# Statistics of y by accumulating passes on ScalarE, and quarters of the image for the first block of k

## The chip, the cores and the metric

One core of a Trainium2 chip runs the whole program. The metric is the device time of the program in microseconds; the time before is a median of three runs.

## The reference

The input is x of 8 images with 384 channels and 64 x 64 positions. Two residual layers follow each other:

- Layer 0: x is normalised over groups of 12 channels. q, k and v are each a 1x1 convolution (384 to 384) and then a depthwise 3x3 convolution. In each of 8 heads of 48 channels, q and k are divided by their norm over the 4096 positions, the 48 x 48 products go through a softmax and are applied to v; a 1x1 convolution follows, and the result is added to x.
- Layer 1: the new x is normalised again over groups, and scanned in four directions with a selective scan of 16 states; the four results are added to y. Then y is normalised over its channels at every position and passed through gelu:

```python
mu = jnp.mean(yc, axis=-1, keepdims=True)
var = jnp.mean((yc - mu) ** 2, axis=-1, keepdims=True)
yc = (yc - mu) * jax.lax.rsqrt(var + LN_EPS) * ln_weight + ln_bias
y = jnp.transpose(yc, (0, 3, 1, 2)).astype(x.dtype)
return jax.nn.gelu(y, approximate=False)
```

and added to x. All is float32.

## The kernel before, in words

The images go one after the other. For each, `channel_attention` makes layer 0 and `selective_scan` makes the scan, which takes most of the time and writes y to DRAM, 4096 positions by 384 channels. The last part of layer 1, the normalisation of y, gelu and the sum, is not made behind the scan of its image but inside the attention of the next image; only that of the last image stands alone at the end, in `finish`.

In the attention the channels lie on the 128 partitions in three blocks (m = 0, 1, 2), each of 4096 columns. `conv` (line 207) makes one block, or some rows of it: TensorE multiplies chunks of 512 columns, three matmuls each (L223), into one of three PSUM buffers; ScalarE evicts each chunk with its bias (L228) into a tile `pre`, which has two buffers, and then multiplies it by the centre weight into the result (L232); VectorE adds the other eight taps (L244). A part of the rows needs one more row on each inner side. The first block of k is made in two halves (line 277), so that VectorE can begin before the whole block is there; blocks 1 and 2 of k are made whole, and so are blocks 0 and 1 of q. After a block, TensorE transposes it and ScalarE copies the transposes out (L268, L269), and ScalarE squares it in eight passes with an accumulator (L255) for the norm, whose small operations on VectorE and ScalarE are L258 to L261; `diag` (L283) spreads it by a matmul. For q, `lg` (L311) holds the logits.

`token_norm` (line 873) makes the mean and the variance of y for each position. It loads y in 16 pieces of 256 positions into a tile with three buffers (L881); VectorE makes two statistics of 384 columns for each piece (L884) and aggregates them (L885); at the end ScalarE takes the root (L886) and VectorE makes the scale and the shift (L887, L888). It is called in the attention of images 1 to 7 ahead of v (line 327), and in `finish` (line 920). `finish_part` (line 891) then applies scale and shift (L900), transposes, applies gelu (L908), adds x (L912) and stores.

In the scan most instructions are held in the order in which they are written. In the attention and in `token_norm` they are not: a scheduler places the instructions of each engine, by their dependences and its own estimates of time, when the program is built. The order that results is fixed, and each engine runs its own instructions in that order. SyncE issues all loads and stores named here, also in a fixed order.

Of the kernel before, what the change touches and what calls it, by code (L numbers as in the profile page):

```python
# [9 lines left out]
F32 = mybir.dt.float32  # L10
AF = mybir.ActivationFunctionType
ALU = mybir.AluOpType
# [3 lines left out]
P = 128  # L16
C = 384
NJ = C // P
H = W = 64
# [3 lines left out]
NT = L // P  # L23
# [31 lines left out]
BW = max(hi - lo for lo, hi in BANDS)  # L55
# [21 lines left out]
def tile_channel_attention_then_selective_scan(ctx: ExitStack, tc: tile.TileContext, a: dict):  # L77
    nc = tc.nc
# [14 lines left out]
    eps = const.tile([P, 1], F32, name="eps")  # L93
# [6 lines left out]
    for name in ("dt_bias", "Ds", "ln_w", "ln_b", "temp"):  # L100
        t = const.tile(list(a[name].shape), F32, name=name)
# [61 lines left out]
    def channel_attention(b, x, stats, before):  # L163
# [5 lines left out]
        with ExitStack() as st:  # L169
            wp = st.enter_context(tc.tile_pool(name=f"w{b}", bufs=1))  # L170
            work = st.enter_context(tc.tile_pool(name=f"a{b}", bufs=2))
# [78 lines left out]
            def inverse_norm(acc, tag):  # L250
                r = work.tile([P, 1], F32, tag="rn", bufs=4, name=f"rn{tag}")
                parts = work.tile([P, L // JUNK], F32, tag="rp", name=f"rp{tag}")
                for i in range(L // JUNK):
                    junk = work.tile([P, JUNK], F32, tag="junk", bufs=1, name=f"junk{tag}_{i}")
                    nc.scalar.activation(  # L255
                        junk, acc[:, bass.ts(i, JUNK)], AF.Square, accum_out=parts[:, i : i + 1]
                    )
                nc.vector.tensor_reduce(r, parts, AX.X, ALU.add)  # L258
                nc.vector.tensor_scalar_max(r, r, L2_EPS * L2_EPS)
                nc.scalar.activation(r, r, AF.Sqrt)  # L260
                nc.vector.reciprocal(r, r)  # L261
                return r

            def to_tokens(acc, t4, out, tag):

                pt = ps_t.tile([P, 4, P], F32, tag="pt", name=f"pt{tag}_{t4}")
                for i in range(4):
                    nc.tensor.transpose(pt[:, i, :], acc[:, bass.ts(4 * t4 + i, P)], ident)  # L268
                nc.scalar.copy(out, pt)  # L269
# [4 lines left out]
            rks = wp.tile([P, C], F32, name=f"rks{b}")  # L274
            for m in range(NJ):
                acc = work.tile([P, L], F32, tag="acc", name=f"ak{b}{m}")
                parts = (0, H // 2, H) if m == 0 else (0, H)
                for y0, y1 in zip(parts, parts[1:]):
                    conv("k", wk, bk, m, y0, y1, acc[:, y0 * W : y1 * W])
                for t4 in range(NT // 4):  # L280
                    to_tokens(acc, t4, kT[:, 4 * t4 : 4 * t4 + 4, bass.ts(m, P)], f"k{b}{m}")
                r = inverse_norm(acc, f"k{b}{m}")
                diag = work.tile([P, P], F32, tag="diag", name=f"diag{b}{m}")  # L283
                nc.vector.tensor_scalar_mul(diag, ident, r)
                pr = ps_a.tile([P, CH], F32, tag="pa", name=f"pr{b}{m}")
                nc.tensor.matmul(pr[:, :P], lhsT=ones, rhs=diag, start=True, stop=True)
                nc.scalar.copy(rks[:, bass.ts(m, P)], pr[:, :P])
# [4 lines left out]
            for m in range(NJ):  # L292
                lo, hi = BANDS[m]
                wd = hi - lo
                acc = work.tile([P, L], F32, tag="acc", name=f"aq{b}{m}")
                parts = (0, H // 2, H) if m == NJ - 1 else (0, H)
                for y0, y1 in zip(parts, parts[1:]):
                    conv("q", wq, bq, m, y0, y1, acc[:, y0 * W : y1 * W])
                pa = ps_a.tile([P, CH], F32, tag="pa", name=f"pa{b}{m}")
                for t4 in range(NT // 4):  # L300
                    qT = work.tile([P, 4, P], F32, tag="qT", name=f"qT{b}{m}_{t4}")
                    to_tokens(acc, t4, qT, f"q{b}{m}")
                    for i in range(4):
                        t = 4 * t4 + i
                        nc.tensor.matmul(
                            pa[:, :wd], lhsT=qT[:, i, :], rhs=kT[:, t, lo:hi],
                            start=t == 0, stop=t == NT - 1,
                        )
                r = inverse_norm(acc, f"q{b}{m}")
                nc.vector.tensor_mul(r, r, small["temp"][:, m : m + 1])  # L310
                lg = work.tile([P, BW], F32, tag="lg", name=f"lg{b}{m}")  # L311
                nc.vector.tensor_mul(lg[:, :wd], pa[:, :wd], rks[:, lo:hi])
                nc.vector.scalar_tensor_tensor(
                    lg[:, :wd], lg[:, :wd], r, mask[:, m, :wd], ALU.mult, ALU.add
                )
                mx = work.tile([P, 1], F32, tag="mx", name=f"mx{b}{m}")
                nc.vector.reduce_max(mx, lg[:, :wd], axis=AX.X)
                nc.vector.tensor_scalar_mul(mx, mx, -1.0)
                sm = work.tile([P, 1], F32, tag="sm", name=f"sm{b}{m}")
                nc.scalar.activation(lg[:, :wd], lg[:, :wd], AF.Exp, bias=mx, accum_out=sm)  # L320
                nc.vector.reciprocal(sm, sm)
                nc.vector.tensor_scalar_mul(attn[:, m, lo:hi], lg[:, :wd], sm)
# [3 lines left out]
            if before is not None:  # L326
                scale, shift = token_norm(b, wp, work, before[2])

                def emit(i):
                    t = work.tile([P, L], F32, tag="acc", name=f"fin{b}_{i}")  # L330
                    room = [t[:, n * FT * NJ : (n + 1) * FT * NJ] for n in range(3)]
                    finish_part(*before, i, scale, shift, room, ps_t, "pt")
# [30 lines left out]
            parts = (0, H // 2, 3 * H // 4, H)  # L363
# [508 lines left out]

    def token_norm(b, keep, work, y_d):

        mv = keep.tile([P, NT, 2], F32, name=f"fmv{b}")
        scale = keep.tile([P, NT], F32, name=f"fsc{b}")
        shift = keep.tile([P, NT], F32, name=f"fsh{b}")
        n = FT // P
        for i in range(L // FT):
            y = work.tile([P, n, C], F32, tag="ft", bufs=3, name=f"fy{b}_{i}")  # L880
            nc.sync.dma_start(y, y_d[bass.ts(i, FT), :].rearrange("(l p) c -> p l c", p=P))  # L881
            for t in range(n):
                stats = work.tile([P, nc.vector.BN_STATS_DIM], F32, tag="fst", name=f"fst{b}_{i}_{t}")
                nc.vector.bn_stats(stats, y[:, t, :])  # L884
                nc.vector.bn_aggr(mv[:, n * i + t, :], stats)  # L885
        nc.scalar.activation(scale, mv[:, :, 1], AF.Sqrt, bias=eps)  # L886
        nc.vector.reciprocal(scale, scale)  # L887
        nc.vector.scalar_tensor_tensor(shift, mv[:, :, 0], -1.0, scale, ALU.mult, ALU.mult)  # L888
        return scale, shift

    def finish_part(b, x1_d, y_d, i, scale, shift, room, psum, tag):
# [23 lines left out]
    def finish(b, x1_d, y_d):  # L915
        with ExitStack() as st:
            wp = st.enter_context(tc.tile_pool(name=f"fw{b}", bufs=1))
            work = st.enter_context(tc.tile_pool(name=f"f{b}", bufs=2))
            ps = st.enter_context(tc.tile_pool(name=f"fp{b}", bufs=4, space=PSUM))
            scale, shift = token_norm(B, wp, work, y_d)  # L920
            for i in range(L // FT):
                room = [
                    work.tile([P, FT * NJ], F32, tag=f"r{n}", bufs=4, name=f"fr{b}_{i}_{n}")
                    for n in range(3)
                ]
                finish_part(b, x1_d, y_d, i, scale, shift, room, ps, "pz")
# [3 lines left out]
    for b in range(B):  # L930
        x1, x1_d, stats1 = channel_attention(b, *x, before)
        y_d, x = selective_scan(b, x1, stats1)
        before = (b, x1_d, y_d)
# [50 lines left out]
```

## Time and profile before

| what | value |
|---|---|
| median of 3 runs | 20560.08 us (20553.85 to 20561.49) |
| profiled execution, its own time | 20559.6 us |
| span of that execution | 20557.8 us, granted TensorE clock 0.968 |
| VectorE busy | 19292.1 us (94%) |
| TensorE busy (matmul) | 19007.6 us (92%) |
| ScalarE busy | 17927.7 us (87%) |
| GpSimd busy | 15434.4 us (75%) |
| statistics of y on VectorE: L884, L885 | 256 of 546 ns (128 loads with two each), 256 of 173 ns |
| taps on VectorE, 128x4032, L244 | 4416 ns each |
| scans on VectorE, L570 | 12288, 1266 or 1230 ns each |

The times of groups are sums over the span, and many lie beside each other on different engines. An image's attention can be found in the profile by the names of its tiles: `ak` is a block of k, `aq` of q, with the image's number in the names of `pre` and `pc` (`pre1k`: image 1). The attention of image 1 begins near 2579 us; the end of the program, where nothing but the last image's normalisation is left, begins near 20453 us. In rows in order of time, the first number is the start in microseconds, the second the duration; brackets hold the idle time of the engine before, and what released it.

### The profile page before, as it was taken

How to read it: one execution, taken by the hardware profiler on the slowest of the kernel's cores; microseconds unless marked ns; L12 is line 12 of the kernel's file. 1: busy time of each engine (PE TensorE's matmuls, PEld its weight loads, DVE VectorE, ACT ScalarE, POOL GpSimd, SP SyncE). 2: the span in 40 equal slices, each digit the busy share in tenths (PEclk: the TensorE clock that was granted, in tenths of full speed). 3: DMA queues.
4: the chain of work that ended last, by engine and by line, in shares of the span. 5: the costliest groups of instructions: out<-in, count | busy, mean ns of one | idle time of the engine just before them, and what ended most of it. 6: DMA issues, size and time to landing. Idle time of an engine off the chain costs nothing. (4 is left out here: it accounts for less than half of the span.)

```text
span 20557.8 us, 319218 instructions
## 1 busy us (share of the span) xinstructions
PE 19007.6 (92%) x118000; PEld 10494.5 (51%) x118000; DVE 19292.1 (94%) x17310; ACT 17927.7 (87%) x32267; POOL 15434.4 (75%) x6918
## 2 busy tenths in 40 slices
PE   7999979999899998999989999899998999989998
PEld 4555545555455554555545555455554555545554
DVE  8999989999899998999989999899998999989998
ACT  3999949999599995999959998599985999859998
POOL 0999809998199981999819997199971999729997
PEclk8999989999899998999989999899998999989999
DMA  1222322223223232222322223222232222322223
GB/s 40 80 91 93 101 77 82 92 92 100 74 83 92 92 104 69 83 91 92 106 69 83 92 92 104 71 83 92 92 102 72 84 92 92 99 74 84 92 92 117
DMA packets 953162, 1807.94 MB, mean 88 GB/s; under 512 B 125904, under 2 KB 646352, under 8 KB 945456
## 3 DMA queue, kind: packets, MB, share of 16 engines
q1 hardware_dynamic: 950736, 1787.40, 27.1%
q8 instruction: 931, 15.25, 0.3%
q14 instruction: 631, 5.17, 0.1%
q10 hardware_dynamic: 864, 0.12, 0.0%
HBM read 1468.39 MB, written 318.77 MB: 87 GB/s over the span
## 5 line engine op out<-in xcount | busy, mean ns | idle before, releaser
L558 POOL TENSOR_TENSOR db<-w,B 128x1536 f32<-128x1536 f32 x4088 | 14145.7, 3470 | 524.1 <-DVE h L570 193.7
L570 DVE TENSOR_TENSOR_SCAN h<-da,ca,db 128x512 f32<-128x512 f32 x10752 | 13030.9, 1266 | 413.8 <-issue 238.2
L604 ACT ACTIVATE hc<-pt,ct 128x384 f32<-128x384 f32 x15128 | 8430.7, 579 | 237.4 <-PE pt L592 176.4
L549 ACT ACTIVATE da<-dt,neg_a 128x512 f32<-128x512 f32 x12288 | 8509.4, 696 | 100.2 <-DVE h L570 66.9
L592 PE MATMUL pt<-ident,h 128*128 128x128 f32 x49152 | 7978.3, 287 | 524.5 <-ACT hc L604 346.0
L592 PEld LDWEIGHTS pt<-ident,h 128*128 128x128 f32 x49152 | 5143.4, 140 | 5174.3 <-ACT hc L604 2506.3
L621 PE MATMUL py<-hc,pair 128*64 128x384 f32 x24576 | 5328.0, 512 | 9.2 <-DVE ys L692 9.2
L406 POOL MEMSET wdt<- 128x1536 f32 x8 | 11.0, 1378 | 3612.3 <-DMA x1d<-x 3612.3
L570 DVE TENSOR_TENSOR_SCAN h<-da,db 128x512 f32<-128x512 f32 x1536 | 1807.3, 1230 | 129.9 <-ACT da L549 61.2
L628 PE MATMUL py<-hc,pair 128*64 128x128 f32 x24576 | 1897.5, 280 | 0.0
L621 PEld LDWEIGHTS py<-hc,pair 128*64 128x64 f32 x24576 | 1215.4, 135 | 1042.6 <-issue 1042.6
L455 PE MATMUL px<-x,wx 128*44 128x128 f32 x6144 | 1502.6, 338 | 35.3 <-ACT x L421 29.1
L628 PEld LDWEIGHTS py<-hc,pair 128*64 128x64 f32 x24576 | 1403.3, 136 | 252.5 <-issue 248.7
L533 POOL TENSOR_TENSOR w<-x,dt 128x512 f32<-128x512 f32 x744 | 1058.1, 1422 | 0.0
L455 PEld LDWEIGHTS px<-x,wx 128*44 128x44 f32 x6144 | 635.0, 121 | 818.1 <-issue 772.6
L584 POOL COPY ca<-h 128x6 f32<-128x6 f32 x1792 | 348.7, 195 | 699.3 <-DVE h L570 690.5
L606 DVE TENSOR_SCALAR hc<-pt,ct 128x384 f32<-128x384 f32 x1256 | 739.0, 605 | 57.2 <-PE pt L592 15.4
L515 PE MATMUL pd<-xd,wdt 128*128 128x512 f32 x1536 | 747.1, 609 | 44.8 <-ACT hc L604 39.0
L353 PE MATMUL pp<-v,mT 128*128 128x512 f32 x1152 | 557.6, 638 | 124.1 <-DVE v L244 57.3
L525 ACT ACTIVATE dt<-pd,dt_bias 128x512 f32<-128x512 f32 x768 | 474.4, 685 | 19.7 <-PE pd L515 16.0
L515 PEld LDWEIGHTS pd<-xd,wdt 128*128 128x128 f32 x1536 | 275.5, 193 | 327.3 <-issue 187.8
L353 PEld LDWEIGHTS pp<-v,mT 128*128 128x128 f32 x1152 | 230.1, 206 | 405.4 <-issue 316.4
(315 smaller groups left out, 11369.7 us busy)
## 6 DMA issues: line engine op xcount, KB each, us to landing
B<-bcd SPq DMA_DIRECT2D x2048, 512.0 KB
yd<-ys SPq DMA_DIRECT2D x128, 576.0 KB
ys<-yd SPq DMA_DIRECT2D x256, 288.0 KB
yd<-ys SPq DMA_DIRECT2D x256, 288.0 KB
x<-in_x SPq DMA_DIRECT2D x48, 1024.0 KB
x1d<-x SPq DMA_DIRECT2D x192, 256.0 KB
fy<-yd SPq DMA_DIRECT2D x128, 384.0 KB
fin<-yd SPq DMA_DIRECT2D x112, 384.0 KB
```

The lines of the kernel that those rows point to most:

```text
L353: nc.tensor.matmul(pc, lhsT=mT[:, j, bass.ts(m, P)], rhs=v[:, j, bass.ts(c, CH)], start=j == 0, stop=j == NJ - 1,)
L455: pin(nc.tensor.matmul(split(pxs[s][:XR, :])[:, part, :], lhsT=wx[:, j, k, :], rhs=view(x1[j], k, c)[:, part, :], start=i == 0, stop=i == ...
L515: pin(nc.tensor.matmul(pds[j], lhsT=wdt[:, k, bass.ts(j, P)], rhs=xds[s], start=True, stop=True))
L533: pin(eng.tensor_mul(split(ws[s][:, j, :]), view(x1[j], k, c), split(dts[s][:, j, :])))
L549: pin(nc.scalar.activation(t, dts[s][:, j, :], AF.Exp, scale=neg_a[:, j, k, n : n + 1]))
L558: pin(eng.tensor_mul(t, ws[g // NP], bts[g][:, v : v + 1, :].broadcast_to([P, NJ, CH])))
L570: pin(nc.vector.tensor_tensor_scan(h, da, db, 0.0 if start else carries[s - 1][:, j, n : n + 1], ALU.mult, ALU.add,))
L592: pin(nc.tensor.transpose(t[:, bass.ts(j, P)], h2s[g][:, j, bass.ts(q, HP), :].rearrange("p l v -> p (l v)"), ident))
L604: pin(eng.activation(out, src, AF.Copy, scale=scale))
L606: pin(eng.tensor_scalar_mul(out, src, scale))
L621: pin(nc.tensor.matmul(py[f * HP : (f + 1) * HP, lb, :C], lhsT=pair, rhs=hc[:, f, :], **flags))
L628: pin(nc.tensor.matmul(py[f * HP : (f + 1) * HP, j, C:], lhsT=pair, rhs=hc[:, f, bass.ts(j, P)], **flags,))
```

## The change

Two things change. The first block of k is made in three parts, two quarters of the image and then the second half, instead of two halves. And in `token_norm` the statistics of VectorE are replaced by passes of ScalarE: for each piece of y, two passes with Identity whose accumulator gives the sum of 384 channels, one multiplication by -1/384 on VectorE for both, and two passes with Square, with minus the mean as bias, whose accumulator gives the sum of the squared deviations. The root at the end takes the division by 384 as its scale. All passes write to one tile `junk` that is not read. The tiles `diag` and `lg` get one buffer instead of two.

```diff
             for m in range(NJ):
                 acc = work.tile([P, L], F32, tag="acc", name=f"ak{b}{m}")
-                parts = (0, H // 2, H) if m == 0 else (0, H)
+                parts = (0, H // 4, H // 2, H) if m == 0 else (0, H)
...
-                diag = work.tile([P, P], F32, tag="diag", name=f"diag{b}{m}")
+                diag = work.tile([P, P], F32, tag="diag", bufs=1, name=f"diag{b}{m}")
...
-                lg = work.tile([P, BW], F32, tag="lg", name=f"lg{b}{m}")
+                lg = work.tile([P, BW], F32, tag="lg", bufs=1, name=f"lg{b}{m}")
...
     def token_norm(b, keep, work, y_d):
 
-        mv = keep.tile([P, NT, 2], F32, name=f"fmv{b}")
...
             nc.sync.dma_start(y, y_d[bass.ts(i, FT), :].rearrange("(l p) c -> p l c", p=P))
+            junk = work.tile([P, C], F32, tag="fj", bufs=1, name=f"fj{b}_{i}")
+            ts = slice(n * i, n * i + n)
             for t in range(n):
-                stats = work.tile([P, nc.vector.BN_STATS_DIM], F32, tag="fst", name=f"fst{b}_{i}_{t}")
-                nc.vector.bn_stats(stats, y[:, t, :])
-                nc.vector.bn_aggr(mv[:, n * i + t, :], stats)
-        nc.scalar.activation(scale, mv[:, :, 1], AF.Sqrt, bias=eps)
+                g = n * i + t
+                nc.scalar.activation(junk, y[:, t, :], AF.Identity, accum_out=shift[:, g : g + 1])
+            nc.vector.tensor_scalar_mul(shift[:, ts], shift[:, ts], -1.0 / C)
+            for t in range(n):
+                g = n * i + t
+                nc.scalar.activation(
+                    junk, y[:, t, :], AF.Square, bias=shift[:, g : g + 1],
+                    accum_out=scale[:, g : g + 1],
+                )
+        nc.scalar.activation(scale, scale, AF.Sqrt, bias=eps, scale=1.0 / C)
         nc.vector.reciprocal(scale, scale)
-        nc.vector.scalar_tensor_tensor(shift, mv[:, :, 0], -1.0, scale, ALU.mult, ALU.mult)
+        nc.vector.tensor_mul(shift, shift, scale)
         return scale, shift
```

In the changed file the multiplication on VectorE is L889, the passes are L888 and L892, and the root is L896.

## The prediction

> **What bounds the kernel now.** I read first the page: busy time and the chain of work that ended last. The chain names ACT, DVE, PE and POOL in the scan, each by a few per cent, so no single engine bounds the whole. The order of instructions in the scan is the same in both programs on all engines (VectorE's 14,248 instructions of that stage, ScalarE's 29,256, and those of PE and SyncE), so I leave the scan at its time and price only the two places that the change touches: the attention at the head of each image and the end of the program.
>
> The attention, read in VectorE's order of time. Image 0 has no statistics of y, image 1 has them; columns are start, duration, engine, line, operation, count and the idle time before it.
>
> ```profile
> 31.83 0.18 DVE L142 RECIPROCAL rstd<-rstd 128x3 f32<-128x3 f32 x1 [0.27 <-ACT rstd L141]
> 53.12 36.49 DVE L244 SCALAR_TENSOR_TENSOR ak<-pre0k,dwk,ak 128x1953 f32<-128x1953 f32 x16 [21.11 <-ACT ak L232]
> 95.58 0.16 DVE L258 TENSOR_REDUCE rnk<-rpk 128x1 f32<-128x8 f32 x1 [5.97 <-ACT junkk L255]
> ...
> 102.21 60.98 DVE L244 SCALAR_TENSOR_TENSOR ak<-pre0k,dwk,ak 128x3969 f32<-128x3969 f32 x14 [5.47 <-ACT ak L232]
> ...
> 174.01 4.35 DVE L244 SCALAR_TENSOR_TENSOR aq<-pre0q,dwq,aq 128x3969 f32<-128x3969 f32 x1 [1.58 <-ACT aq L232]
> ```
>
> ```profile
> 2599.11 1.02 DVE L884 BATCH_NORM_STATS2 fst<-fy 128x6 f32<-128x384 f32 x2 [0.79 <-DMA fy<-yd]
> 2600.34 2.25 DVE L244 SCALAR_TENSOR_TENSOR ak<-pre1k,dwk,ak 128x1953 f32<-128x1953 f32 x1 [0.20 <-ACT ak L232]
> ...
> 2640.70 0.55 DVE L884 BATCH_NORM_STATS2 fst<-fy 128x6 f32<-128x384 f32 x1
> ...
> 2649.61 60.98 DVE L244 SCALAR_TENSOR_TENSOR ak<-pre1k,dwk,ak 128x3969 f32<-128x3969 f32 x14 [3.16 <-ACT ak L232]
> ...
> 2720.88 13.20 DVE L244 SCALAR_TENSOR_TENSOR aq<-pre1q,dwq,aq 128x3969 f32<-128x3969 f32 x3 [1.05 <-ACT aq L232]
> ```
>
> See that from the first tap of k to the first tap of q image 0 takes 174.01 - 53.12 = 120.9 us without statistics and image 1 takes 2720.88 - 2600.34 = 120.5 us with them. VectorE's statistics therefore cost nothing here: they lie in the 20 us before the first tap and in the gap before block 1 of k. What sets both waits is the chain PE, eviction (L228), centre tap (L232): block 1 starts at 102.21 and 2649.61, 49.1 and 49.3 us after the first tap, though the taps of block 0 take only 36.5 us. The reason is the two buffers `pre`: ScalarE can evict for block 1 only when the first half is released.
>
> The end of the program, VectorE's and ScalarE's order of time:
>
> ```profile
> 20464.50 1.02 DVE L884 BATCH_NORM_STATS2 fst<-fy 128x6 f32<-128x384 f32 x2 [8.84 <-DMA fy<-yd]
> ...
> 20493.47 0.30 DVE L885 BATCH_NORM_AGGREGATE fmv<-fst 128x2 f32<-128x6 f32 x2
> ```
>
> ```profile
> 20452.84 1.28 ACT L886 ACT_TABLE_LOAD   x1
> 20493.81 0.32 ACT L886 ACTIVATE fsc<-fmv,eps 128x32 f32<-128x32 f32 x1 [39.68 <-DVE fmv L885]
> 20494.98 1.91 ACT L900 ACTIVATE fr<-fr,fsh,fsc 128x384 f32<-128x384 f32 x3 [0.85 <-DVE fsh L888]
> ```
>
> Here nothing covers the statistics: from 20464.50 to 20493.81, 29.3 us for 16 loads of y, ScalarE only waits (39.68 us), with its table for Sqrt already in.
>
> **What the Trainium skill says.** "ScalarE: Activation LUTs", section "What ACT_TABLE_LOAD costs": an ACTIVATE with immediate scale and bias takes 186 + 0.833 N ns, a pointer operand adds about 93 ns, and successive ones overlap by about 93 ns; a table load takes 1283 ns and a drain of about 1380 ns follows. The trace agrees on the first: the accumulating Square at L255 over 512 columns has a mean of 632 to 649 ns against 613 estimated. It agrees on the 1283 ns; no drain of 1380 ns shows (the load at 20496.90 is followed by an ACTIVATE at 20498.20). The page does not price the accumulator; the trace does (next part).
>
> **The change, part by part.**
>
> *1. A pass with accumulator.* No row has it at 384 columns. L255 at 512 columns:
>
> ```profile
> 2639.66 0.63 ACT L255 ACTIVATE junkk<-ak 128x512 f32<-128x512 f32 x1 [0.78 <-DVE fmv L885]
> 2640.20 0.19 ACT L255 ACTIVATION_READ_ACCUMULATOR junkk<-ak 128x1 f32 x1
> 2640.42 0.63 ACT L255 ACTIVATE junkk<-ak 128x512 f32<-128x512 f32 x1
> ```
>
> So one with its read takes 0.76 us from start to start. 128 columns fewer are 0.107 us (slope of L232: (3.71 - 2.00)/2048 = 0.835 ns per column): 0.65 us for the sum pass, and 0.75 for the Square with its pointer bias (an estimate with that page's 93 ns). Mean 0.70; bounds 0.60 and 0.85 (the L255 of 512 columns with a pointer). Per image 64 passes, 45 us of ScalarE.
>
> *2. Image 0: quarters alone.* The first quarter needs 17 rows: two chunks of 512 and one of 64. Chunks leave PE every 2.57 us; the second one's eviction is at 45.12, the small one's follows to 46.1, the tap over 1024 columns takes 1.15 (L232 in v): first tap at 47.3 instead of 53.12, 5.8 us earlier. Sixteen taps of 1.27 (the 128x1008 rows of v), some overlapping, end about 67.2. The price: one more chunk, of 128 columns, and eight more taps at half size, whose fixed cost is in these 1.27 us (two of 1008 against one of 2016 at 2.25 to 2.31). The third part needs the first quarter's buffer (free at about 60), but its evictions stand behind the q bias, which waits for PE to about 61.6; its centre tap ends about 69.4, so VectorE stands 2 us and ends block 0 at 87.5. Block 1 takes the second quarter's buffer, free at 67.2 (before: the first half's, about 78); PE's chunks then run to 88.7, two transposes' evictions and a Square follow, the centre tap ends at 95.5. Block 1 starts 102.2 - 95.5 = 6.7 us earlier. The norm's small operations (0.8 us), before in the gap, now stand between taps: 5.9 us won.
>
> *3. Images 1 to 7: quarters with the passes.* ScalarE's order now has 7 passes before the first centre tap, 4.9 us. They fit beside PE, which delivers the chunks at 2589.8 and 2592.3: first centre tap ends at 2595.0, 5.3 us before 2600.34. From the third part's tap (ends about 2616.5) to block 1's tap there stand 18 passes, 6 evictions, 4 Squares and 5 copies: 12.6 + 4.2 + 2.8 + 2.8, with the last wait on VectorE and the tap's 3.71: I follow it item by item to 2644.9, against 2649.6: 4.7 us. VectorE's removed statistics (32 of 0.546 and 32 of 0.173 us, 23 us) give nothing, as image 0 against image 1 shows. It gets 16 multiplications of 128x2 instead (0.15 us, as L259), each waiting for two passes; queued behind each are the taps, and PE's transposes wait for those. Eight stand before block 1's start, in slack; eight after it cost 1.2; the norm's operations 0.8; short waits for the pass where the multiplications of y loads 13 and 14 stand in q's taps 0.3. 4.7 - 2.3 = 2.4 us per image, 16.8 for seven. Bounds: 0.5 and 5.3 (the whole first lead).
>
> Of what moves: SyncE's loads of y now wait for ScalarE's passes, the last ones in q's block 1 instead of by 2630; queued behind are the load of wv (now ahead of the last four, needed about 2665, released about 2656) and those of the first finished parts, which start at 2808.99. So nothing. Single buffers for `diag` and `lg`: their matmul and softmax are done tens of us before the next, 0; if one were late, under 1 us. Table loads: 578 in both.
>
> *4. The end.* ScalarE makes all 64 passes alone: per load 2 x 0.65 + 2 x 0.75 = 2.8, and once to VectorE and back: 0.15 with about 0.15 of waking (between 0.03 and 0.24 by the gaps at 20494): 3.1 us. 16 x 3.1 = 49.6 against 29.3: +20.3. The Sqrt table load now stands behind the passes, in the open: +1.3. In all +21.6. The loads of y do not bind: 16 of them and 8 for the parts to finish went out from 20461 to 20489 before, 1.2 us each. The 60 us of finishing that follow keep their order. Bounds 16 (passes at 0.60, 0.2 of waking) and 27 (0.85 on half of them, 0.45).
>
> *Sum.* -5.9 - 16.8 + 21.6 = -1.1 us on the profiled execution's 20559.6 us (its span 20557.8 and 1.8 around it). That execution is 0.5 us under the median 20560.08; 20559 us for the median after.
>
> **The rivals.**
> - A, the sum as above: 20559, chance 0.66.
> - B, the lead is kept whole: 5.3 in each of seven images, 6.7 in image 0, the end only 16 us longer: -28, 20532. For it: block 1 waits on a chain that begins earlier. Against: ScalarE's passes are in that chain. Chance 0.22.
> - C, VectorE is what bounds the attention and all that is taken from it counts: after the first tap of image 1 stand about 7.4 us of statistics (10 of 0.546, 11 of 0.173), with the lead 12.7 us per image: -88.9 - 5.9 + 21.6 = -73, 20487. Against: image 0 takes the same time without statistics. Chance 0.06.
> - D, slower: ScalarE is the new bound, at the multiplications and in block 1's chain. With passes of 1.0 us, the 7 + 18 passes on the chain add 7.5 per image: -2.4 becomes +5.1, 36 for seven, the end 21.6 + 19 = 41, image 0 -5.9: +71, 20631. It loses over 0.2% from a pass of about 0.88 us on ((41 + 1)/(64 + 7 x 25) = 0.18 over my 0.70). For it: from 2616 to 2645 the items above leave ScalarE hardly a gap. Against: L255 shows 0.76 at more columns. Chance 0.06.
>
> That the program does not do what is said is excluded by its order of instructions.
>
> **How the numbers follow.** The likeliest is A. The ends of the range: -7 x 5.3 - 6.7 + 16 = -28 (B), and -7 x 0.5 - 3 + 27 = +21, so 20532 to 20581; C and D, 0.12, are outside. 0.2% is 41 us, about what a measurement of this kernel can tell from no change; A and B lie within it: same 0.88, faster 0.07 (C and a little of B), slower 0.05 (D).
>
> **What would show it.** Right: image 0's first tap about 47 and block 1 about 95.5; in image 1, counted from the reciprocal at L142 (2579.91), the first tap at about 15 us instead of 20.4 and block 1 at about 65 instead of 69.7; the stretch of passes at the end about 50 us with a table load after it; passes near 0.54 us with a 0.19 us read. Wrong: passes over 0.85 us, waits of VectorE at L889 of more than 1 us per image, block 1 not earlier, or a scan that has changed.

## The result, and the profile after

The changed kernel takes 20518.01 us (median of 15 runs, 20507.59 to 20528.97), the kernel before beside it on the same chips 20554.01 us (15 runs, 20552.33 to 20561.87): ratio 0.9981, 95% interval 0.9974 to 0.9987, 36 us faster. The forecast was 20559 us with a range from 20532 to 20581. The gain of 0.18% still lies within the 0.2% that the prediction called "same", but the time lies below its range. Of the 41 us between forecast and result, 6 are the kernel before: the forecast was worked out from a median of 20560, and beside the result it has 20554. Taken from 20554, the range would begin at 20526, still above the result. The profiled execution took 20519.27 us, its span is 20517.5; that is 40.3 us less than the span before, where the sum in the prediction had 1.1.

VectorE's order of time in the changed kernel, first image 0 and then image 1 (start, duration, engine, line, operation, count, and in brackets the wait before it with its releaser):

```profile
31.69 0.18 DVE L142 RECIPROCAL rstd<-rstd 128x3 f32<-128x3 f32 x1 [0.27 <-ACT rstd L141]
46.94 13.41 DVE L244 SCALAR_TENSOR_TENSOR ak<-pre0k,dwk,ak 128x945 f32<-128x945 f32 x11 [15.08 <-ACT ak L232]
...
93.38 4.35 DVE L244 SCALAR_TENSOR_TENSOR ak<-pre0k,dwk,ak 128x3969 f32<-128x3969 f32 x1 [6.61 <-ACT ak L232]
...
164.41 4.35 DVE L244 SCALAR_TENSOR_TENSOR aq<-pre0q,dwq,aq 128x3969 f32<-128x3969 f32 x1 [0.66 <-ACT aq L232]
...
2568.73 0.18 DVE L142 RECIPROCAL rstd<-rstd 128x3 f32<-128x3 f32 x1 [1.68 <-ACT rstd L141]
2576.70 0.17 DVE L889 TENSOR_SCALAR fsh<-fsh 128x2 f32<-128x2 f32 x1 [7.80 <-ACT fj L888]
...
2583.57 2.46 DVE L244 SCALAR_TENSOR_TENSOR ak<-pre1k,dwk,ak 128x945 f32<-128x945 f32 x2 [2.59 <-ACT ak L232]
...
2626.11 0.17 DVE L889 TENSOR_SCALAR fsh<-fsh 128x2 f32<-128x2 f32 x1 [1.06 <-ACT fj L888]
2634.05 4.35 DVE L244 SCALAR_TENSOR_TENSOR ak<-pre1k,dwk,ak 128x3969 f32<-128x3969 f32 x1 [7.77 <-ACT ak L232]
...
2642.77 0.15 DVE L259 TENSOR_SCALAR rnk<-rnk 128x1 f32<-128x1 f32 x1
2642.84 0.16 DVE L889 TENSOR_SCALAR fsh<-fsh 128x2 f32<-128x2 f32 x1
2642.90 4.35 DVE L244 SCALAR_TENSOR_TENSOR ak<-pre1k,dwk,ak 128x3969 f32<-128x3969 f32 x1
...
2706.57 13.20 DVE L244 SCALAR_TENSOR_TENSOR aq<-pre1q,dwq,aq 128x3969 f32<-128x3969 f32 x3 [2.13 <-ACT aq L232]
```

See that image 0 has its first tap of k at 46.94 (before 53.12), block 1 at 93.38 (102.21) and q at 164.41 (174.01). In image 1, counted from L142, the first tap comes 14.8 us after it (before 20.4), block 1 at 65.3 (69.7) and q at 137.8 (141.0). The wait in front of block 1 is still one for ScalarE's centre tap, L232.

ScalarE's order of time at the end of the program:

```profile
20404.65 0.52 ACT L888 ACTIVATE fj<-fy 128x384 f32<-128x384 f32 x1 [11.59 <-DMA fy<-yd]
...
20405.29 0.52 ACT L888 ACTIVATE fj<-fy 128x384 f32<-128x384 f32 x1
...
20406.14 0.61 ACT L892 ACTIVATE fj<-fy,fsh 128x384 f32<-128x384 f32 x1 [0.23 <-DVE fsh L889]
...
20406.88 0.61 ACT L892 ACTIVATE fj<-fy,fsh 128x384 f32<-128x384 f32 x1
...
20452.25 1.28 ACT L896 ACT_TABLE_LOAD   x1
20453.54 0.32 ACT L896 ACTIVATE fsc<-fsc,eps 128x32 f32<-128x32 f32 x1
```

The passes run from 20404.65 to 20452.25, 47.6 us where VectorE needed 29.3, and the table load stands after them, in the open. From the start of the last addition of ys, the scan's last sum on VectorE, to the end of the span it is 122.3 us, before 102.8.

The stretch that the prediction didn't look at lies between them: from v's last tap to the scan's first h (L570). Two windows of the changed kernel, images 2 and 3; the column after POOL's is the granted TensorE clock:

```profile
5542.40:5583.80 41.40, 29.79 (x108) 19.30 (x108) 23.61 (x46) 12.91 (x17) 3.99 (x4) 0.76 0.32 102
8093.00:8130.80 37.80, 26.54 (x108) 16.42 (x108) 23.59 (x46) 12.91 (x17) 4.13 (x4) 0.84 0.33 113
```

The same 108 matmuls, the same VectorE and ScalarE work, and 3.6 us apart: what differs is the clock, and TensorE's busy time with it. Here are two groups of that stretch (the last matmuls of the second group norm, L136, and the scan's first projection, L455), in the kernel before (image 1) and in the changed one (images 2 and 3):

```profile
3020.18 3.15 PE L136 MATMUL pv<-var,avg 128*128 128x1 f32 x14 [0.84 <-DVE var L131]
3026.93 5.35 PE L455 MATMUL px<-x,wx 128*44 128x128 f32 x24 [3.61 <-ACT x L421]
```

```profile
5560.68 3.15 PE L136 MATMUL pv<-var,avg 128*128 128x1 f32 x14 [0.84 <-DVE var L131]
5567.43 5.15 PE L455 MATMUL px<-x,wx 128*44 128x128 f32 x24 [3.61 <-ACT x L421]
...
8110.35 1.90 PE L136 MATMUL pv<-var,avg 128*128 128x1 f32 x14 [0.84 <-DVE var L131]
8115.85 4.13 PE L455 MATMUL px<-x,wx 128*44 128x128 f32 x24 [3.60 <-ACT x L421]
```

Fourteen small matmuls take 3.15 us in images 1 to 7 of the kernel before, all seven. In the changed kernel they do so in images 1, 2 and 7; in images 3 to 6 they take 1.72 to 1.90. TensorE alone over these matmuls, in image 1 of the kernel before and in image 4 of the changed one (busy time, then the granted clock):

```profile
3020.18:3023.33 3.15, 3.15 (x14) 0.50 0.00 0
```

```profile
10656.32:10658.04 1.72, 1.72 (x14) 1.00 0.03 8
```

So the record of the clock has half where they are slow and full where they are fast. The Trainium skill, "TensorE: Matmul & The Clock Gate", section "Part 1: The HAM clock gate (the "warmup" mystery)", says that the clock is either half or full, and is set from TensorE's activity in a free-running window of 3.4 us. The two durations of L136 and the two clocks beside them agree with two levels, and the times at which the record changes agree with the window (steps of 3.413 us, below); whether the level depends on TensorE's activity is tested in the experiments.

All marks together, in us: for images 1 to 7 the mean start from L142 of k's first tap, block 1 of k, the first tap of q, v's last tap ("v ends"), and the first h; then the scan, from the first h to the last addition of ys. "End" is the stretch from image 7's last addition of ys to the end of the span. "Again" is a second profile of the same kernel.

| kernel | k | block 1 | q | v ends | h | scan | end |
|---|---|---|---|---|---|---|---|
| before | 20.8 | 70.3 | 141.7 | 423.0 | 464.4 | 2072.2 | 102.8 |
| before, again | 21.4 | 71.1 | 142.6 | 425.0 | 465.6 | 2071.9 | 101.8 |
| after | 15.4 | 64.5 | 136.6 | 419.0 | 458.6 | 2070.9 | 122.3 |
| after, again | 15.0 | 64.6 | 136.7 | 419.1 | 458.6 | 2072.0 | 122.2 |
| quarters alone | 14.9 | 62.6 | 133.8 | 416.4 | 457.6 | 2072.0 | 101.1 |
| statistics alone | 21.4 | 70.9 | 142.7 | 426.2 | 466.4 | 2071.7 | 121.0 |
| after, VectorE at the end | 15.3 | 64.2 | 136.2 | 418.2 | 458.3 | 2070.8 | 102.7 |

So the 40.3 us between the first profiles of before and after (the first pair) are: image 0 up to the L142 of image 1, 11.2; the attention of images 1 to 7 to v's last tap, 27.7 (4.0 each); from there to h, 12.9 (1.8 each); their scans, 9.6; less 19.4 at the end and 1.6 between one scan and the next L142. The second pair ("again") differs by 37.5, in the same order: 10.5, 41.2 (5.9 each), 7.9, -0.5, less 20.4 and 1.2. The kernel before alone differs between its two profiles by 2.0 us at v's last tap, so a difference of 1 or 2 us per image between single profiles can be scatter.

Quarters alone have nothing of the gain between v and h: 41.3 us. Statistics alone have 40.2.

### The profile page after: what moved, and what is told of

It reads as the page before. It is cut to its first block, busy times and chain, and to the rows that moved or that the text cites. A ratio compares the mean times of both kernels' runs of the same rounds, so it can differ in the third digit from the quotient of the medians.

```text
span 20517.5 us, 320069 instructions
## 1 busy us (share of the span) xinstructions
PE 18992.4 (93%) x118048; PEld 10487.8 (51%) x118048; DVE 19167.9 (93%) x16990; ACT 18228.0 (89%) x33307; POOL 15433.8 (75%) x6918
## 5 line engine op out<-in xcount | busy, mean ns | idle before, releaser
L570 DVE TENSOR_TENSOR_SCAN h<-da,ca,db 128x512 f32<-128x512 f32 x10752 | 13032.6, 1267 | 411.8 <-issue 236.7
L570 DVE TENSOR_TENSOR_SCAN h<-da,db 128x512 f32<-128x512 f32 x1536 | 1807.7, 1230 | 125.7 <-ACT da L549 54.9
L455 PE MATMUL px<-x,wx 128*44 128x128 f32 x6144 | 1498.1, 337 | 35.1 <-ACT x L421 28.8
L455 PEld LDWEIGHTS px<-x,wx 128*44 128x44 f32 x6144 | 632.1, 121 | 817.3 <-issue 772.5
```

The lines of the kernel that those rows point to most:

```text
L455: pin(nc.tensor.matmul(split(pxs[s][:XR, :])[:, part, :], lhsT=wx[:, j, k, :], rhs=view(x1[j], k, c)[:, part, :], start=i == 0, stop=i == ...
L570: pin(nc.vector.tensor_tensor_scan(h, da, db, 0.0 if start else carries[s - 1][:, j, n : n + 1], ALU.mult, ALU.add,))
```

## The experiments

Ratios are to the kernel before on the same chip. Two sets of runs, the first four experiments and the rest, stand against 20554 and 20565 to 20567 us, so ratios are compared, not times.

**Quarters alone.**

```diff
 # the kernel before
-                parts = (0, H // 2, H) if m == 0 else (0, H)
+                parts = (0, H // 4, H // 2, H) if m == 0 else (0, H)
```

> Quarters alone; the statistics of y stay on VectorE as before, diag and lg stay double. Theory (the gain is the earlier chain of k, kept whole, and a TensorE clock that no longer falls in k; ScalarE's passes only cost): all that the change won in the attention stays and the 19.5 us lost at the end come back, so about 20518 - 19.5 = 20498 us (20485 to 20515), first tap of k about 15 us after L142 and block 1 about 62 to 65 in every image. Rival (what was won in images 1 to 7 is VectorE's freed time): only image 0's 11 us stay and a us or so per further image, about 20535 to 20543.

Measured: 20499.53 us, ratio 0.9974 [0.9965, 0.9984]. VectorE in image 1, and at the end:

```profile
2629.97 1.00 DVE L884 BATCH_NORM_STATS2 fst<-fy 128x6 f32<-128x384 f32 x2
2631.26 4.35 DVE L244 SCALAR_TENSOR_TENSOR ak<-pre1k,dwk,ak 128x3969 f32<-128x3969 f32 x1 [0.28 <-ACT ak L232]
...
2702.53 13.19 DVE L244 SCALAR_TENSOR_TENSOR aq<-pre1q,dwq,aq 128x3969 f32<-128x3969 f32 x3
...
20405.56 1.02 DVE L884 BATCH_NORM_STATS2 fst<-fy 128x6 f32<-128x384 f32 x2 [8.93 <-DMA fy<-yd]
...
20432.81 0.30 DVE L885 BATCH_NORM_AGGREGATE fmv<-fst 128x2 f32<-128x6 f32 x2
```

VectorE's statistics fill its gap in front of block 1 to the last 0.28 us and leave none in front of q. Quarters alone gain more than the whole change, with VectorE's statistics in place; the rival (VectorE's freed time) falls.

**Statistics alone.**

```diff
 # the changed kernel
-                parts = (0, H // 4, H // 2, H) if m == 0 else (0, H)
+                parts = (0, H // 2, H) if m == 0 else (0, H)
```

> Statistics on ScalarE alone, block 0 of k in halves as before. Theory: nothing is won in the attention, since ScalarE's passes stand in block 1's chain (0 to 5 us lost in each of seven images), and the end costs 19.5 us: 20573 to 20610 us. Rival (freed VectorE time is the gain): about 4 us won in each of seven images, 20554 - 28 + 19.5 = 20546 us.

Measured: 20584.39 us, ratio 1.0016 [1.0009, 1.0022], 30 us slower. ScalarE ahead of block 1 of k in image 1:

```profile
2639.67 0.61 ACT L892 ACTIVATE fj<-fy,fsh 128x384 f32<-128x384 f32 x1
...
2640.41 0.52 ACT L888 ACTIVATE fj<-fy 128x384 f32<-128x384 f32 x1
...
2641.08 0.69 ACT L228 ACTIVATE pre1k<-pc1k,bias1k 128x512 f32<-128x512 f32 x1
2641.66 0.52 ACT L888 ACTIVATE fj<-fy 128x384 f32<-128x384 f32 x1
...
2642.16 3.70 ACT L232 ACTIVATE ak<-pre1k,dwk 128x4096 f32<-128x4096 f32 x1
```

Passes stand right in front of the centre tap that VectorE waits for. The cost that is clear is the 18 to 19 us at the end of the program. In the attention this kernel is later than the first profile of before by 1.0 us at q and 3.2 at v's last tap, but than the second by 0.1 and 1.2, which scatter can make. Beside quarters alone the passes show better: the changed kernel is 0.5 us later at the first tap, 1.9 at block 1, 2.8 at q and 2.7 at v's last tap, 19 us in seven images, and its second profile agrees (0.1, 2.0, 2.9, 2.7). By the medians, quarters give 55 and statistics take 30: 25 us, against 36 measured together. That rest of 11 us isn't clear of noise. It is about what the changed kernel gains between v and h beside quarters alone (12 us), but no run ties the two together.

**The last statistics back on VectorE.**

```diff
 # the changed kernel; token_norm_v is the token_norm of before
-            scale, shift = token_norm(B, wp, work, y_d)
+            scale, shift = token_norm_v(B, wp, work, y_d)
```

> The changed kernel, but the last image's statistics (nothing beside them) made on VectorE with bn_stats as before; the seven others stay on ScalarE. Both theories: the end falls from 122.3 us to about 103, so 20518 - 19.5 = 20498 us; another time by more than 8 us would say that the end's cost reaches further back.

Measured: 20498.45 us, ratio 0.9973 [0.9963, 0.9983]; the end takes 102.7 us. The cost at the end is local, and as large as said.

**Keeping TensorE busy in the second norm, first try.**

```diff
 # the changed kernel, norm_factors, for the second norm only: 4 matmuls, then 12
+        for _ in range(4):
+            nc.tensor.matmul(pm[:, P : 2 * P], lhsT=ident, rhs=ident, start=True, stop=True)
         nc.vector.tensor_copy(mean, pm[:, 0:NJ])
...
+        for _ in range(12):
+            nc.tensor.matmul(pv[:, P : 2 * P], lhsT=ident, rhs=ident, start=True, stop=True)
         nc.vector.tensor_scalar_add(rstd, pv[:, 0:NJ], GN_EPS)
```

> The changed kernel with 4 + 12 matmuls of 128 columns, whose results nobody reads, behind the two small groups of matmuls of the second group norm (L124, L136), where TensorE has next to nothing to do. Theory (the 41.4 us of images 1, 2 and 7 against 38 of images 3 to 6, from v's last tap to the scan's first h, is the granted clock, which falls there): all seven images take 38 us or less, 10 us in all, 20508 us. Rival (the clock is not the cause, or the record of it is noise): 41.4 stays in some images and the added matmuls cost 0 to 2 us each, 20518 to 20530 us.

Measured: 20578.22 us, 1.0011 [1.0005, 1.0018]: 60 us more than the changed kernel, a miss of both theories. VectorE and TensorE in image 1:

```profile
3015.02 0.16 DVE L128 COPY mean<-pm 128x3 f32<-128x3 f32 x1 [3.27 <-PE pm L128]
...
3023.42 0.16 DVE L140 TENSOR_SCALAR rstd<-pv 128x3 f32<-128x3 f32 x1 [7.66 <-PE pv L140]
```

```profile
3012.93 2.05 PE L128 MATMUL pm<-ident 128*128 128x128 f32 x8
...
3018.83 4.55 PE L140 MATMUL pv<-ident 128*128 128x128 f32 x24
```

VectorE's reads of pm and pv (L128, L140) wait for the last of the added matmuls, which write other columns of the same tile; the stretch from v's last tap to h takes 46.1 us instead of 39.6. The run tells of that wait and nothing of the clock. The next ones give the unread matmuls a tile of their own, and keep their place in TensorE's order.

**Keeping TensorE busy, in a tile of its own.** In the first norm, on quarters alone:

```diff
 # fill(n): n matmuls of ident with ident into pw, kept in program order, as pm's and pv's are
+            pw = ps_a.tile([P, CH], F32, tag="pa", name=f"pw0{b}")
+            fill(26)
             mean, rstd = norm_factors(wp, ps_m, stats, f"0_{b}", "misc", dict(tag="wt", bufs=2))
 # and within it: fill(2) behind pm's matmuls, fill(8) behind pv's
```

> Quarters alone (as e1_quarters, 20499.5 us), with 26 + 2 + 8 matmuls that nobody reads put on TensorE ahead of, between and behind the two small groups of matmuls of the first group norm of each image (L124, L136), in a PSUM tile of their own. Theory (the clock that is down when k begins costs time, because k's first block is bound by TensorE now): L124 and L136 take 1.7 us instead of 3.1, the bias matmuls and the first chunk about 2 us less, so 4 to 5 us per image for seven images: 20465 us (20460 to 20480), block 1 of k about 58 us after L142. Rival (the granted clock has no part in it): 20499 us or, since the 26 take up to 13 us at the low clock, up to 20535.

Measured: 20470.94 us, 0.9953 [0.9941, 0.9966]; block 1 comes 59.1 us after L142 (62.6 in quarters alone). TensorE in image 3:

```profile
7632.73 6.07 PE L177 MATMUL pw<-ident 128*128 128x128 f32 x52
7645.90 3.12 PE L124 MATMUL pm<-mv,avg 128*128 128x1 f32 x14 [7.10 <-DMA mask<-in_mask]
...
7656.49 0.42 PE L199 MATMUL pb3k<-mean,wk 128*128 128x1 f32 x2
7656.77 1.59 PE L223 MATMUL pc3k<-x,wk 128*128 128x512 f32 x2
```

The 26 fill only 6 of 13 us, and L124 is still slow; the matmuls behind the norm are faster (L223 1.59 us for two, at a recorded clock of 0.69; 2.06 in quarters alone, at 0.50). Added work that computes nothing makes the kernel faster, and the clock over the same matmuls is higher. This run also keeps pm's and pv's matmuls in program order, and no run does that without the fill, so a part of the gain may be the order's.

In the second norm, on quarters alone:

```diff
+                pw = ps_m.tile([P, CH], F32, tag="m", name=f"pw1{b}")
                 mean, rstd = norm_factors(np_, ps_t, stats1, f"1_{b}", "t")
 # within it: fill(2) behind pm's matmuls, fill(8) behind pv's
```

> Quarters alone (as e1_quarters, 20499.5 us), with 2 + 8 unread matmuls behind L124 and L136 of the second group norm only, in a PSUM tile of their own, so that VectorE doesn't wait for them as it did in e4_warm. Theory (41.5 us from v's last tap to the first h are a clock that falls there, 38 are one that doesn't): 38 us in all seven images, 7 x 3.3 = 23 us less, about 20477 us. Rival: 41.5 stays, or the eight hold up the projection behind them at the low clock by 1.5 us per image: 20500 to 20511.

Measured: 20482.52 us, 0.9960 [0.9948, 0.9973]. Image 1:

```profile
3003.23 3.15 PE L136 MATMUL pv<-var,avg 128*128 128x1 f32 x14
3006.24 3.44 PE L413 MATMUL pw<-ident 128*128 128x128 f32 x16
3009.98 2.82 PE L455 MATMUL px<-x,wx 128*44 128x128 f32 x24 [0.30 <-ACT x L421]
```

The first projection takes 2.82 us instead of 5.35 in five of the seven images, and 3.43 and 3.83 in the others. L136 stays slow, so the stretch to h falls from 41.3 to 39.7 us and not to 38: right in kind, half in size. (The interval overlaps that of quarters alone; the durations at L455 don't.)

**The first quarter begun by eighths.**

```diff
 # quarters alone
-                parts = (0, H // 4, H // 2, H) if m == 0 else (0, H)
+                parts = (0, H // 8, H // 4, H // 2, H) if m == 0 else (0, H)
```

> Quarters alone, but the first quarter begun by two eighths of the image. Theory (with quarters TensorE has no gap left from the first chunk of k to block 1, so block 1 is bound by TensorE's work): the first tap comes 2.6 us earlier and block 1 no earlier, perhaps 1 us later for the one more chunk: 20499 us (20495 to 20508). Rival (block 1 hangs on the chain that begins with the first tap, as before the change): 2.6 us in each of eight images, 20478 us.

Measured: 20458.39 us, 0.9951 [0.9937, 0.9964]. Counted from L142 and against quarters alone, the first tap comes 2.7 us earlier and block 1 still 1.3 (61.2), so my theory (bound by TensorE, no gain) falls. The rival's 21 us are too few as well: the end of v comes 4.1 us earlier, 3.4 of them between the first taps of q and of v; the reason stays open.

**A delay of known length.**

```diff
 # the kernel before
             mean, rstd = norm_factors(wp, ps_m, stats, f"0_{b}", "misc", dict(tag="wt", bufs=2))
+            for _ in range(6):
+                nc.vector.tensor_scalar_mul(rstd, rstd, 1.0)
```

> The kernel before with six multiplications of rstd by 1.0 behind L142, which is on every image's path: about 1.2 us per image. If times add up plainly: 8 x 1.2 = +9.6, 20564 us. Theory (TensorE's clock changes only on a grid of 3.41 us, and the image's length in the kernel before, 2556.58 us = 749 steps, hangs on it): the delay is swallowed, 0 to +3 us, or costs a whole step per image, +20 us or more.

Measured: 20578.52 us, 1.0006 [0.9998, 1.0014], 13 us by the medians. That is near the plain sum (9.6), and the mean first tap comes 1.2 to 1.8 us later than in the two profiles of before, so the delay isn't swallowed there. But the interval reaches from 4 us less to 29 us more, so the time alone rules out neither a delay that costs nothing nor a whole step of the clock per image.

**The two kernels once more.** The changed kernel and the kernel before, unaltered, profiled again.

> The changed kernel once more, unaltered. Theory (22 of its 36 us, in the stretch between v and the scan and in the scan's first 80 us, hang on where a fall of TensorE's clock lies, which shifts by the length of what came before): again about 0.18% faster than before with a spread of 15 to 20 us, L136 of the second norm at 1.72 us in some images and 3.15 in others, not necessarily the same ones. Rival (those gains belong to the change's own instructions): the same four images at 38 us from v to h, and 0.18% again.

> The kernel before, profiled a second time. If the fall of the clock in the second norm belongs to the length of what comes before it there, L136 takes 3.15 us again in all seven of images 1 to 7 and v to h 41.3 to 41.6; if it is chance, some images have 1.72 us and 38.

Measured: 20531.42 us beside 20566.89, ratio 0.9983 [0.9977, 0.9990]; the second profile of before is a single run of 20564.89. In the second profile of the changed kernel L136 is fast in images 2, 3, 5 and 6, not in 3 to 6; two of its images:

```profile
3006.88 3.15 PE L136 MATMUL pv<-var,avg 128*128 128x1 f32 x14 [0.84 <-DVE var L131]
...
5560.13 1.80 PE L136 MATMUL pv<-var,avg 128*128 128x1 f32 x14 [0.84 <-DVE var L131]
```

The second profile of before has it slow in five images, at 1.72 in image 5 and 2.11 in image 7; v to h has a mean of 40.7 us (41.4 in the first), the changed kernel 39.5 (39.6). So the fall is more frequent before, not a fixture of it: of 12.9 us in the first pair of profiles, 7.9 are left in the second, and of the scan's 9.6 nothing (2071.9 and 2072.0).

The record of the clock tells which images are hit. In all 16 profiles of this case every stretch between two of its changes, but for the last in a profile, lasts a whole number of steps of 3.413 us. Where L124's first matmul in the second norm starts up to 8.05 us after the last rise to full clock, the clock falls three steps after that rise, and L136 takes 3.13 to 3.15 us. Where it starts 8.06 us or more after, the clock falls four steps after the rise, and L136 takes 1.72 to 2.62. All 128 images obey this. In images 1 to 7 that start lies 7.40 to 7.73 us after the rise in the kernel before, 7.89 to 8.50 in the changed one, and 7.73 to 8.73 and 7.80 to 8.53 in their second profiles: a shift of some tenths of a microsecond decides. What shifts it isn't shown. It isn't the passes on ScalarE alone: of images 1 to 7, L136 is fast in 14 of 28 in four profiles with them and in 5 of 35 in five without, but in 4 of 7 with eighths, which have none.

**Single buffers.**

```diff
 # quarters alone
-                diag = work.tile([P, P], F32, tag="diag", name=f"diag{b}{m}")
+                diag = work.tile([P, P], F32, tag="diag", bufs=1, name=f"diag{b}{m}")
 # and lg likewise
```

> Quarters alone, with diag and lg of a single buffer as the change has them. All theories: as e1_quarters, 0.9974 of before (20499 us beside 20554), since nobody waits for either; over 5 us more would be a wait for diag or lg.

Measured: 20504.22 us, 0.9970 [0.9959, 0.9981]; quarters alone had 0.9974. No cost, as forecast.

**The clock alone, on both kernels.** The second norm's fill, as above, on the kernel before and on the changed one:

> The kernel before, unchanged in k and in its statistics, with 2 + 8 unread matmuls in the second group norm only. Theory (what the change won between v and the scan and in the scan's beginning is clock and nothing else): the first px (L455) takes 2.8 us instead of 5.35, 1.8 us less from v to h and 1.4 us in the scan, 7 x 3.2 = 22 us less than before, ratio 0.9989. Rival (it needs k's or the statistics' change): 1.000, or up to 1.0005 for the added matmuls.

> The changed kernel with 2 + 8 unread matmuls in the second group norm, in a PSUM tile of their own (what e4_warm meant to be). Theory: the first px takes about 2.8 to 3.8 us in every image, 39 to 40 us from v to h where it is 41.4 now and about 38 to 39 where the clock doesn't fall anyway, the scan at 2070 to 2071 us in all images: 5 to 12 us less than the change alone, ratio 0.9976 to 0.9980. Rival: no gain over the change alone, 0.9981 to 0.9986.

Measured: 20550.87 us on the kernel before, 0.9992 [0.9984, 1.0001]; 20514.51 on the changed one, 0.9975 [0.9965, 0.9984], where the change alone has 0.9981 and 0.9983. Image 1 of the latter:

```profile
3004.55 0.69 PE L413 MATMUL pw<-ident 128*128 128x128 f32 x4
3005.53 1.72 PE L136 MATMUL pv<-var,avg 128*128 128x1 f32 x14 [0.29 <-DVE var L131]
3007.11 3.54 PE L413 MATMUL pw<-ident 128*128 128x128 f32 x16
3010.85 2.82 PE L455 MATMUL px<-x,wx 128*44 128x128 f32 x24 [0.20 <-ACT x L421]
```

From v to h the changed kernel's mean falls from 39.6 to 38.3 us, before's from 41.4 (40.7 in its second profile) to 39.3, and L455 takes 2.8 to 3.7 us in every image of both. The recorded clock over L455 is 0.75 to 1.00 there in images 1 to 7, and 0.50 to 0.67 in the two kernels without the fill: the clock does follow what TensorE is given to do. Without any change in k or in the statistics, then, that stretch is shorter by 1.4 to 2.1 us per image; the 16 us by the medians aren't clear of noise (the interval just reaches 1). The scan's mean didn't fall as expected (2071.9 in the changed kernel with the fill).

**The best version.** Eighths and a quarter, statistics on VectorE, and both fills (52 + 2 + 8 and 2 + 8).

> The best version in sight: the first block of k begun by two eighths and a quarter, statistics on VectorE as before the change, and unread matmuls in both group norms (52 + 2 + 8 in the first, since 26 filled 6 of 13 idle us in e5_warm_norm0; 2 + 8 in the second). If the gains of e5, e6 and e7 against e1 (28, 17 and 41 us by the medians) added up, 20499 - 86 = 20413; L124 and L136 of the first norm at 1.7 instead of 3.1 us would give another 2.8 us in each of seven images, 20393. Theory: 20385 to 20435 us. Rival (the gains are the same windows counted thrice): no better than the best of them, 20450.

Measured: 20431.68 us, 0.9936 [0.9923, 0.9948], better than both kernels. The gains of the three parts over quarters alone are 0.0021, 0.0014 and 0.0023, in sum 0.0058; 0.0038 came, so they don't add up.

## Why the prediction was wrong, point by point

- **A pass with accumulator** (part 1): right. 0.65 us from start to start for the sum (20404.65, 20405.29) and 0.74 for the Square (20406.14, 20406.88), as worked out from L255.
- **The end** (part 4): right in kind, 1 to 2 us too dear. Each load takes 2.98 us and not 3.1, so 16 take 47.6; the table load of 1.28 us is exposed as said. 19.4 us instead of 21.6 (20.4 in the second pair).
- **Image 0** (part 2): the first tap is right (46.94; said 47.3). Block 1 was put at 95.5 and came at 93.38. One item that failed is "PE's chunks then run to 88.7": the last of block 1's eight evictions starts at 87.49, so its chunk had left TensorE before that. With a shorter wait at q (0.66 us, before 1.58) 9.6 us are won at q instead of 5.9, and 11.2 by the end of the image.
- **Images 1 to 7, "4.7 - 2.3 = 2.4 us per image"** (part 3): the first lead is right (5.4; said 5.3), and this step failed. Block 1's lead is 5.8 and not 4.7, and the deduction of 2.3 from there to q was 0.75 (0.65 in the second pair). The price of the multiplications was too high: from the start of one tap over 4032 columns to the next it is 4.329 us with nothing between, 4.448 with L889, 4.454 with L259 (in the kernel before), and 4.465 with both (medians). So one between two taps costs 0.12 us, or 0.01 beside another small operation, and not the 0.15 of its own duration, because VectorE's operations overlap there (2642.84 to 2642.90). The lead kept at q is 5.0 us of 5.4. Of it 1.0 is lost by v's last tap, but not to the passes: quarters alone lose 1.2 there beside the same profile, and beside the second profile of before neither loses any. The net is 4.0 us per image, 27.7 for seven, where the sum has 16.8; in the second pair it is 5.9, 41.2 for seven.
- **"I leave the scan at its time and price only the two places that the change touches"**: this step failed too, and it is the one that a reader should keep. The same order of instructions is not the same time: 12.9 us (7.9 in the second pair) came between v and the scan, where no line was changed, because TensorE's clock fell there in fewer images. That it is the clock is shown by L136 and L455 (same operands, two durations, with the recorded clock at half or full beside them), by its moving to other images in a second profile, and by three kernels in which unread matmuls shorten the projection at L455. Which image would be hit could not have been forecast, since 0.01 us on one side or the other of 8.05 decides; that this stretch has a swing of 3 to 4 us per image, about 25 us in all (an estimate from 41.4 and 37.8 us), could have been, from its mean clock of 0.75, and belonged in the range.
- **Which of the two was larger** depends on the pair. Image 0 and the attention give 16 us more than the sum in the first pair and 29 in the second; what was held constant gives 22.5 and 7.4. Without what was held constant the spans would differ by 18 us in the first pair, within the range, and by 30 in the second, 2 beyond its lower end of 28; what was held constant brought it well below in the first pair and further below in the second.
- **The rivals.** B (the lead is kept whole, 20532) came nearest: at q 5.0 us of 5.4 are kept per image. C (VectorE's freed time) falls with quarters alone, which are faster with VectorE's statistics in place. D's mechanism, ScalarE's passes in block 1's chain, exists in small: 2.7 us per image beside quarters alone, with passes of 0.65 and 0.74 us and not of 1.0. It is not what decides. Of the signs named for being wrong, two came: waits of VectorE at L889 (7.80 and 1.06 us in image 1), behind which it waits for the centre tap as well (2.59 and 7.77), so these two set nothing; and, in the first pair alone, a changed scan.

What stays open: the scan's 9.6 us of the first pair. The scans of all kernels here lie between 2068.9 and 2074.0 us without a clear owner, and the second pair shows no difference; I take it for the scatter of single profiles. Nor is it settled why the attention's gain is 4.0 us per image in one pair and 5.9 in the other; the clock in k, q and v is a likely cause, but no run isolates it.

## What to carry to other kernels

Where a chain begins with a piece of work, cut its first piece smaller: 55 us came from one line, and eighths gave more. Statistics that lie in an engine's gaps need not be moved: on ScalarE, which heads the chain, they cost 30 us by themselves, 18 to 19 of it in the one place that has no cover, while quarters gained 55 us with them left on VectorE. And where TensorE waits between small groups of matmuls, read the granted clock of that stretch before holding it constant: a shift of some tenths of a microsecond upstream can change it, and unread matmuls in a tile of their own can keep it up.

## What was not expected of the hardware

- The 14 matmuls of one column at L136 take 3.15 us where the recorded clock is 0.50 and 1.72 where it is 1.00, with values in between where it changes under them (2.11 us at 0.78 in image 7 of the second profile of before). Which it is hangs on where the norm starts on a grid of 3.413 us, to within 0.01 us. The Trainium skill, "TensorE: Matmul & The Clock Gate", section "HAM oscillation — how this bites in real kernels", tells of matmuls that start slow again after each wait; here it is at most 3.6 us in this place, and the mean clock of 0.88 from L142 to v's last tap (image 1 of the kernel before) says that it isn't the only one.
- In this program a read of a tile waited for all that was written to it: VectorE's read of three columns of pm stood idle for 3.27 us until matmuls into other columns, earlier in the program, were done.
- An operation of VectorE of 0.15 to 0.16 us between two long taps adds 0.12 us, and a second one beside it 0.01.
